# Sums and zero counts of the weights: from VectorE and GpSimd on one layout to ScalarE on another

## The chip, the cores and the metric

The kernel runs on one core of a Trainium2 chip, as a single program. The metric is the device time of one execution in microseconds (us). One execution was also recorded by the hardware profiler; its span runs from its first to its last instruction. PE is TensorE, DVE is VectorE, ACT is ScalarE, POOL is GpSimd, SP is the engine that issues most of the DMAs.

## The reference

A batch of 16 images with 256 channels of 28 x 28 goes through four layers, each with its input added at the end:

```python
# layer 0
out = _binary_activation(x)                       # values sign(x)
scaling = mean(abs(weights), axis=(1, 2, 3))      # one per output channel
y = conv3x3(out, sign(weights)) * scaling
x = batchnorm(y, gamma, beta) + x                 # moments over the batch
# layer 1
x = ...   # 3x3 and 1x1 convolutions of sign(x + move) with real weights (a_w, f_w),
          # PReLU, batch norms with given moments, two squeeze-and-excite gates
# layer 2
sf = mean(abs(w), axis=(1, 2, 3), keepdims=True)  # for w1 and for w2
out = sign(batchnorm(x, g1, b1))
out = prelu(conv3x3(out, sf1 * sign(w1)), a1)
out = sign(batchnorm(out, g2, b2))
out = prelu(conv3x3(out, sf2 * sign(w2)), a2)
x = prelu(batchnorm(out, g3, b3) + x, a3)
# layer 3
x = attention(x) + x                              # 784 tokens, 64 wide, softmax
```

The change concerns the three binary weight tensors, w0, w2a (`w1` of layer 2) and w2b (`w2` of layer 2), each 256 x 256 x 3 x 3. Of each the kernel needs the signs, the mean of |w| for every output channel (sf0, sf1, sf2, which enter the batch norms only through epsilon), and whether any weight is exactly zero: the fast path packs two output channels into one number and relies on signs of +1 and -1. If a zero or another doubt turns up, a flag makes the kernel run a second, careful path; with the inputs here it isn't run.

## The kernel before

Weights reach the chip as `taps`: for each half k of the input channels an array of 128 input channels by 9 taps by 256 output channels. They are loaded in six pieces of 128 x 768, (k, g), g being a row of taps.

`sign_weights` makes two lists of steps from them. A `sign` step lets ACT write the signs (L269, tile `sg`) and DVE pack two halves of the output channels into `wpk` (L270). An `add_up` step lets POOL compare the piece with zero and add the result up in `zeros` (L278, L279), and DVE sum |w| over the three taps (L285, tile `ab`) and add it to `sums` (L135, which is the line of a helper for all tensor_tensor operations). After the sixth piece, `total_up` sums over the partitions with two matmuls (L297, `sumabs`) and scales (L298). For layer 2 `both` joins a sign and an add_up step on the same piece.

`sign_layer` runs a binary convolution image by image, in an order written by hand on PE, ACT, DVE and SP. For image j: 36 matmuls (L350); signs of image j+1 into `fpads` on ACT (L461 in layer 0, L1051 in layer 2), with two pads in turn; bn_stats of image j-1 (L597, or PReLU and bn_stats at L1085 and L1087); then, from image 1 on, two entries of the list `steps`, one for each half image; then `apart`, in which ACT rounds the packed sums (L361, tile `t`) and takes the rounding off (L362), and DVE gets the other half by subtraction (L364, tile `n` in layer 0, `ab` in layer 2). PSUM has three buffers `cv`. The work that a step returns is run in the next slot, before that slot's own step.

In layer 0 the list holds: six `w1_step`s, which make layer 1's weights (DVE L511, L135 tile `asm`, L521; ACT L520, in turns), the `add_up` steps of w0 (whose six pieces stay in SBUF from the start), `fw_step`, `constants` (small DVE operations on the batch norms), and the six joint steps for w2a. Steps load their pieces two steps ahead into three buffers `x2`. In layer 2's first convolution the list holds the six joint steps for w2b.

Layer 1 is a loop `iteration(b)` over images, in hand-written order on PE, DVE and ACT; SP's order is the scheduler's. Per iteration PE takes a `cv` buffer six times: four pairs of 3x3 convolutions (L693) and two of the 1x1 convolution (L803). `rows_out` (DVE L733, tile `y`) empties the fourth pair. Near the end of an iteration ACT does two `squares2` (L834); at the start of the next it empties the 1x1 results (`unit_u`, L816, tile `u`). DVE's `branch2` (L825) and `transform` (L135, tile `vs`) stand between.

`doubts_so_far` (L1396 to L1399), near the end of layer 3, reduces `zeros` and the other doubts for the flag.

Of the kernel before, what the change touches and what calls it, by code (L numbers as in the profile page):

```python
# [27 lines left out]
F32 = mybir.dt.float32  # L28
FR = mybir.dt.float32r
F16 = mybir.dt.float16  # L30
BF16 = mybir.dt.bfloat16
# [8 lines left out]
P = 128  # L40
# [43 lines left out]
def forward(ctx: ExitStack, tc: tile.TileContext, d: dict, out: bass.AP, careful: bool):  # L84
# [42 lines left out]
    if not careful:  # L127
        zeros = const.tile([P, 3, 256], BF16, name="zeros")
        nc.gpsimd.memset(zeros, 0.0)
# [125 lines left out]
    def sign_weights(pool, dst, src, total, acc, stage=("st", 2), tmp=None, ab_tag="rn", sg=("sg", 1), deferred=None):  # L255


        sts, all_ = {}, []
        tmp = tmp or pool

        def load(k, g):
            if (k, g) not in sts:
                sts[k, g] = load_taps(pool, src, k, g, *stage)

        def sign(k, g):
            st = sts[k, g]
            n = CHUNKS.index((k, g))
            t = tmp.tile([P, 3, 256], BF16, tag=sg[0], name="sg", bufs=sg[1])
            A.activation(t, st, AF.Sign, saturate=False)  # L269
            return lambda: V.scalar_tensor_tensor(  # L270
                dst[:, n], t[:, :, P:], PACK, t[:, :, 0:P], ALU.mult, ALU.add
            )

        def add_up(k, g):
            st = sts.pop((k, g))
            if not careful:
                zero = const.tile([P, 3, 256], BF16, tag="zero", name="zero", bufs=1)
                nc.gpsimd.tensor_scalar(zero, st, 0.0, None, ALU.is_equal)  # L278
                nc.gpsimd.tensor_tensor(zeros, zeros, zero, ALU.add)  # L279
            if not all_:  # L280
                all_.append(tmp.tile([P, 256], F32, tag="total", name="sums", bufs=1))
                ab = all_[0]
            else:
                ab = tmp.tile([P, 256], F32, tag=ab_tag, name="ab", bufs=2)
            V.tensor_reduce(ab, st.rearrange("p t o -> p o t"), AX.X, ALU.add, apply_absolute_value=True)  # L285
            if ab is not all_[0]:
                tt(all_[0], all_[0], ab, ALU.add)
            if (k, g) == CHUNKS[-1]:
                if deferred is None:
                    return lambda: total_up()()  # L290
                deferred.append(total_up)
            return lambda: None

        def total_up():
            part = acc.tile([P, 2], F32, tag="sm", name="sumabs")
            for mo in range(2):
                T.matmul(part[:, mo:mo + 1], lhsT=all_[0][:, mo * P:(mo + 1) * P], rhs=ones, start=True, stop=True)  # L297
            return lambda: V.tensor_scalar(total, part, 1.0 / K9, None, ALU.mult)  # L298

        return [[Step(lambda c=c: load(*c), lambda c=c, f=f: f(*c)) for c in CHUNKS] for f in (sign, add_up)]  # L300

    def both(first, second):
        def work(f, s):
            rest = f.work(), s.work()
            return lambda: [r() for r in rest]

        return [Step(f.load, lambda f=f, s=s: work(f, s)) for f, s in zip(first, second)]
# [122 lines left out]
    with tc.tile_pool(name="ps_conv", bufs=3, space=PSUM) as psc, \  # L430
# [13 lines left out]
        with tc.tile_pool(name="ph1", bufs=1) as ph:  # L444
# [31 lines left out]
            signs, sums_ = sign_weights(ph, w0, d["w0"], sf0, pss, ("yu", 6), sg=("t1", 2))  # L476
# [106 lines left out]
            last_sum = []  # L583
            signs2, sums2 = sign_weights(xpool, w2a, d["w2a"], sf1, pss, ("x2", 3), tmp=ph, deferred=last_sum)
            steps = load_ahead(steps + both(signs2, sums2), 2)

            for i, x in enumerate(sums_):
                steps[3 * i + 1:3 * i + 1] = [x.work, None]
            steps[19:19] = [constants, None]
            steps[-5:-5] = [None]  # L590
            steps[-2:-2] = [None]
# [15 lines left out]

            with tc.manual_schedule(engines={ET.PE}):
                total_up = last_sum[0]()
# [23 lines left out]
            vs = ph.tile([P, 2, 4, 2, HR, S + 2], FR, tag="vs", name="vs")  # L633

# [211 lines left out]
            def iteration(b):  # L846
# [89 lines left out]
            with tc.manual_schedule(engines={ET.PE, ET.DVE, ET.Activation}):  # L936
# [13 lines left out]
                total_up()  # L950
# [83 lines left out]
        with tc.tile_pool(name="ph2", bufs=1) as ph:  # L1034
# [75 lines left out]
            steps = both(*sign_weights(xpool, w2b, d["w2b"], sf2, pss, ("x2", 3), tmp=ph, ab_tag="sums"))  # L1110
# [52 lines left out]
    attend_unshifted(tc, d, out, wqk, wv, wp, keys, worst, (doubts, zeros), flag, pv, finish)  # L1163
# [43 lines left out]
def attend_unshifted(ctx, tc, d, out, wqk, wv, wp, keys, worst, doubts, flag, pv, finish):  # L1207
# [510 lines left out]
```

## Time and profile before

| | us |
|---|---|
| median of 3 runs | 1015.17 |
| lowest and highest | 1012.84, 1019.25 |
| the profiled execution | 1017.7 |
| its span | 1015.4 |
| PE, DVE, ACT, POOL busy in the span | 972.5, 819.0, 632.4, 212.0 |
| layer 0 (start to the first matmul of layer 1) | 0 to 137.77 |
| layer 1 (to the first L350 of layer 2) | 137.77 to 509.37 |
| layer 2, first convolution | 509.37 to 621.99 |
| layer 2, second convolution | 621.99 to 734.03 |
| layer 3 | 734.03 to 1015.4 |

The stage borders are starts of matmuls in PE's timeline. The span is shorter than the execution's own time by 2.3 us. The busy time of PE is that of pipelined matmuls and doesn't say that it ran at its peak. The mean granted clock was 0.985 of full speed.

### The profile page before, as it was taken

What the parts mean: (1) busy time and instruction counts of PE and PEld (TensorE: products, weight loads), DVE (VectorE), ACT (ScalarE), POOL (GpSimd) and SP (SyncE); (2) the same over time, 40 slices, a digit from 0 to 9 for tenths busy, and PEclk for the clock granted to TensorE, in tenths of its full rate; (3) what the DMA queues carried; (4) which work ended last, traced back from release to release, by engine and by line L of the source; (5) the groups of instructions that cost most, each with busy time, mean ns of one, the idle gap of its engine ahead of it and who ended that gap; (6) DMA issues with size and microseconds to landing.
All of it is one profiled execution on the core that took longest, in us unless ns stands there. A gap on an engine that the chain in (4) does not pass through costs nothing. (4 is left out here: it accounts for less than half of the span.)

```text
span 1015.4 us, 14615 instructions
## 1 busy us (share of the span) xinstructions
PE 972.5 (96%) x5627; PEld 668.3 (66%) x5627; DVE 819.0 (81%) x1356; ACT 632.4 (62%) x1003; POOL 212.0 (21%) x186
## 2 busy tenths in 40 slices
PE   7898889999999999999999998999999999999996
PEld 3454569999999999999655554555444444444442
DVE  5997898998999998997769985888856776867775
ACT  5665444656566565665678865777576676666652
POOL 9423500000000000000043100000034444353521
PEclk9998999999999999999999999999999999999999
DMA  9666521222223222100194100000031534334312
GB/s 343 235 220 197 187 80 49 80 94 81 80 80 112 111 81 95 64 34 32 68 360 158 48 33 1 1 1 1 1 65 33 127 73 119 85 107 96 96 64 99
DMA packets 24354, 98.73 MB, mean 97 GB/s; under 512 B 3202, under 2 KB 6980, under 8 KB 24276
## 3 DMA queue, kind: packets, MB, share of 16 engines
q1 hardware_dynamic: 18356, 66.36, 18.5%
q0 software_dynamic: 5632, 30.54, 10.9%
q8 instruction: 46, 0.75, 0.3%
q10 hardware_dynamic: 288, 0.80, 0.2%
q14 instruction: 32, 0.26, 0.1%
HBM read 65.59 MB, written 32.11 MB: 96 GB/s over the span
## 5 line engine op out<-in xcount | busy, mean ns | idle before, releaser
L350 PE MATMUL cv<-fpads,wpk 128*128 128x392 f16 (+1 forms) x1746 | 304.3, 337 | 13.5 <-ACT fpads L1051 4.1
L693 PE MATMUL cv<-vs,w 128*128 128x392 f32 x1536 | 303.0, 355 | 3.0 <-DVE vs L135 3.0
L693 PEld LDWEIGHTS cv<-vs,w 128*128 128x128 f32 x1536 | 288.1, 191 | 5.8 <-issue 3.5
L350 PEld LDWEIGHTS <-wpk 128*128 128x128 f16 x1746 | 172.5, 99 | 145.3 <-issue 21.0
L1300 ACT ACTIVATE es<-sc 128x784 f32<-128x784 f32 x112 | 87.4, 822 | 41.9 <-PE sc L1296 41.7
L1296 PE MATMUL sc<-q,keyswa 64*128 64x392 f32 x448 | 89.9, 513 | 0.9 <-ACT es L1300 0.9
L831 POOL DMA_DIRECT2D x2d<-x x16 | 8.6, 536 | 359.9 <-DVE x L825 295.3
L1317 PE MATMUL av<-es,v 128*64 128x392 f32 x448 | 80.8, 499 | 0.0
L361 ACT ACTIVATE t<-cv,rounding 128x784 f32<-128x784 f32 (+2 forms) x52 | 44.6, 858 | 47.2 <-PE cv L350 46.5
L1085 DVE SCALAR_TENSOR_TENSOR p<-ab,vec 128x784 f32<-128x784 f32 (+1 forms) x68 | 69.4, 1020 | 1.2
L1310 POOL TENSOR_TENSOR sum<-sum,es 128x784 f32<-128x784 f32 x32 | 67.2, 2100 | 3.1 <-ACT es L1300 0.6
L1296 PEld LDWEIGHTS sc<-q,keyswa 64*128 64x128 f32 x448 | 38.9, 186 | 44.0 <-issue 17.1
L135 DVE TENSOR_TENSOR vs<-pad 128x840 fp32r<-128x840 bf16 (+1 forms) x66 | 64.4, 1000 | 0.1
L1317 PEld LDWEIGHTS av<-es,v 128*64 128x64 f32 x448 | 29.6, 136 | 47.1 <-issue 46.9
L364 DVE SCALAR_TENSOR_TENSOR ab<-ab,cv 128x784 f32<-128x784 f32 (+1 forms) x34 | 31.2, 917 | 36.3 <-ACT ab L362 36.3
L1284 DVE COPY keyswa<-mi 64x392 f32<-64x392 f32 x31 | 16.3, 565 | 52.6 <-ACT q L1280 52.6
L714 ACT ACTIVATE t<-cv,c_bn,s_bn 128x392 f32<-128x392 f32 x32 | 21.7, 678 | 52.9 <-PE cv L693 52.9
L803 PE MATMUL cv<-z,fw 128*128 128x392 f32 x256 | 49.1, 343 | 1.0 <-ACT z L795 0.9
L816 ACT ACTIVATE u<-cv,c_bn,s_bn 128x784 f32<-128x784 f32 x30 | 30.1, 1005 | 30.7 <-PE cv L803 30.6
L1308 POOL TENSOR_TENSOR sum<-es 128x784 f32<-128x784 f32 x16 | 30.0, 1878 | 91.0 <-ACT es L1300 91.0
L1273 PE MATMUL mi<-p,wqk 128*128 128x392 f32 x124 | 45.7, 509 | 2.2 <-DVE p L1260 2.1
L278 POOL TENSOR_SCALAR zero<-st 128x768 bf16<-128x768 f32 x18 | 39.2, 2179 | 40.5 <-DMA st<-in_w2b_dram 33.2
(287 smaller groups left out, 1531.9 us busy)
## 6 DMA issues: line engine op xcount, KB each, us to landing
xs<-in_x_dram SPq DMA_DIRECT2D x30, 784.0 KB, 4.4
x2d<-x POOLq DMA_DIRECT2D x16, 784.0 KB, 3.6
out_dram<-p SPq DMA_DIRECT2D x15, 784.0 KB, 3.5
p<-x2d POOLq DMA_DIRECT2D x14, 784.0 KB, 6.7
p<-x2d SPq DMA_DIRECT2D x13, 784.0 KB, 9.3
n0d<-n POOLq DMA_DIRECT2D x16, 392.0 KB, 4.2
n<-n0d SPq DMA_DIRECT2D x16, 392.0 KB, 3.0
st<-in_w_dram SPq DMA_DIRECT2D x12, 384.0 KB, 6.7
```

What stands on the lines that cost most here:

```text
L135: V.tensor_tensor(o, a, b, op)
L278: nc.gpsimd.tensor_scalar(zero, st, 0.0, None, ALU.is_equal)
L350: T.matmul(pss[j][:, n // size if careful else h, :rows * S].rearrange("p (a b) -> p a b", b=S), lhsT=w[:, n, t, :], rhs=pads[:, blocks[j] ...
L361: A.activation(by_halves(t, blocks[j]), ps, AF.Identity, bias=rounding, scale=1.0 / PACK)
L693: T.matmul(ps.rearrange("p (a b) -> p a b", b=S), lhsT=w[:, k, c, u, mo * P:(mo + 1) * P], rhs=vs[:, b % 2, u, k, :, c:c + S], start=(n == 0),
L803: T.matmul(ps[:, h, :HN], lhsT=w[:, k, mo * P:(mo + 1) * P], rhs=z2[b][:, k, h * HN:(h + 1) * HN], start=(k + i == 0), stop=(k + i == 2),)
L1085: V.scalar_tensor_tensor(p, y, alpha[:, mo:mo + 1], y, ALU.mult, ALU.max)
L1273: T.matmul(ps[:, h, :HN], lhsT=wqk[:, k, :], rhs=x[b][:, k, h * HN:(h + 1) * HN], start=(k == 0), stop=(k == 1))
L1296: T.matmul(ps[:, h, :HN], lhsT=chunk[rows], rhs=qs[b][rows], start=True, stop=True)
L1300: A.activation(e, ps[:, :, :HN], AF.Exp, scale=0.125)
L1310: (V if late else nc.gpsimd).tensor_tensor(sums[b, late], sums[b, late], e, ALU.add)
L1317: T.matmul(ps[64 * h:64 * h + 64, :HN], lhsT=w, rhs=e[:, h, :], start=start, stop=stop)
```

## The change

The weights are given to the chip a second time, as rows: two halves of 128 output channels by 2304. `weight_sums` loads them in six pieces of 128 x 768. On each, ACT computes |w| with an accumulator, which gives a sum for each output channel, and then the sign of the result, again with an accumulator, which counts the nonzero weights (`nonzero`, 18 columns). Both write over the piece. After the sixth piece DVE adds three partial sums per channel and scales. The comparison on POOL, the sums on DVE and the matmuls over partitions are gone.

The sums of w0 become steps of layer 0, which run in threes: a w1 step, a sum step of w0, a sign step of w2a. With the empty entries that are put in, an image with a w1 step and an empty slot alternates with an image that has a sum and a sign step, from image 1 to image 12; `fw_step` and `constants` follow at image 13. In before the w2a steps came after `fw_step` and `constants`. The sums of w2a and w2b are done in layer 1: iteration b loads a piece into one of two buffers `sts`, and iteration b+1 works on it, for b from 0 to 11, after the squares and before `transform`. The last piece of each tensor runs `add_up` on DVE at that place, in iterations 6 and 12.

In the compiled order SP issues the loads of the first two pieces of w2a's rows in layer 0. On POOL only the comparisons and additions are missing; the stores of `n` stand in the same order.

```diff
-    if not careful:
-        zeros = const.tile([P, 3, 256], BF16, name="zeros")
-        nc.gpsimd.memset(zeros, 0.0)
+    PIECE = K9 // 3
+    nonzero = None if careful else const.tile([P, 18], F32, name="nonzero")
...
-        def add_up(k, g):
-            st = sts.pop((k, g))
-            if not careful:
-                zero = const.tile([P, 3, 256], BF16, tag="zero", name="zero", bufs=1)
-                nc.gpsimd.tensor_scalar(zero, st, 0.0, None, ALU.is_equal)
-                nc.gpsimd.tensor_tensor(zeros, zeros, zero, ALU.add)
...
-            V.tensor_reduce(ab, st.rearrange("p t o -> p o t"), AX.X, ALU.add, apply_absolute_value=True)
-            if ab is not all_[0]:
-                tt(all_[0], all_[0], ab, ALU.add)
...
+        return [Step(lambda c=c: load(*c), lambda c=c: sign(*c)) for c in CHUNKS]
+
+    def weight_sums(room, src, total, at):
+        parts = const.tile([P, 2, 3], F32, name=f"abs_{at}")
+        sts = {}
+
+        def load(mo, q):
+            st = sts[mo, q] = room()
+            nc.sync.dma_start(out=st, in_=src[mo, :, q * PIECE:(q + 1) * PIECE])
+
+        def work(mo, q):
+            st = sts.pop((mo, q))
+            A.activation(st, st, AF.Abs, accum_out=parts[:, mo, q:q + 1])
             if not careful:
+                n = at + 3 * mo + q
+                A.activation(st, st, AF.Sign, accum_out=nonzero[:, n:n + 1])
+            if (mo, q) == (1, 2):
+                return add_up
             return lambda: None
 
-        def total_up():
-            part = acc.tile([P, 2], F32, tag="sm", name="sumabs")
-            for mo in range(2):
-                T.matmul(part[:, mo:mo + 1], lhsT=all_[0][:, mo * P:(mo + 1) * P], rhs=ones, start=True, stop=True)
-            return lambda: V.tensor_scalar(total, part, 1.0 / K9, None, ALU.mult)
...
+        def add_up():
+            V.tensor_reduce(total, parts, AX.X, ALU.add)
+            V.tensor_scalar(total, total, 1.0 / K9, None, ALU.mult)
...
-            signs2, sums2 = sign_weights(xpool, w2a, d["w2a"], sf1, pss, ("x2", 3), tmp=ph, deferred=last_sum)
-            steps = load_ahead(steps + both(signs2, sums2), 2)
-
-            for i, x in enumerate(sums_):
-                steps[3 * i + 1:3 * i + 1] = [x.work, None]
-            steps[19:19] = [constants, None]
-            steps[-5:-5] = [None]
-            steps[-2:-2] = [None]
+            def room_sums():
+                return xpool.tile([P, PIECE], F32, tag="x2", name="sts", bufs=3)
+
+            signs2, sums0 = sign_weights(xpool, w2a, d["w2a"], ("x2", 3), tmp=ph), weight_sums(room_sums, d["w0_rows"], sf0, 0)
+            steps = [s for three in zip(steps, sums0, signs2) for s in three] + steps[6:]
+            steps = load_ahead(steps, 2)
+            steps[19:19] = [constants]
+            for i in range(6):
+                steps[4 * i + 1:4 * i + 1] = [None]
...
-            with tc.manual_schedule(engines={ET.PE}):
-                total_up = last_sum[0]()
             keep_busy(28)
...
+            sums12 = weight_sums(room_sums, d["w2a_rows"], sf1, 6) + weight_sums(room_sums, d["w2b_rows"], sf2, 12)
...
                     load_x(b + 2, True)
+                if b < len(sums12):
+                    sums12[b].load()
...
                         squares2(b - 2, k)
+                if one and b <= len(sums12):
+                    sums12[b - 1].work()()
                 if ahead:
                     transform(b + 1, 0)
...
-            steps = both(*sign_weights(xpool, w2b, d["w2b"], sf2, pss, ("x2", 3), tmp=ph, ab_tag="sums"))
+            steps = sign_weights(xpool, w2b, d["w2b"], ("x2", 3), tmp=ph)
...
-        V.tensor_reduce(some, doubts[1], AX.XY, ALU.max)
-        V.scalar_tensor_tensor(sure, some, 0.0, sure, ALU.is_le, ALU.mult)
+        V.tensor_reduce(some, doubts[1], AX.X, ALU.min)
+        V.scalar_tensor_tensor(sure, some, K9 / 3.0, sure, ALU.is_ge, ALU.mult)
...
+        "w0_rows": get("L0_conv_weights").reshape(2, P, K9),
+        "w2a_rows": get(L2 + "w1").reshape(2, P, K9),
+        "w2b_rows": get(L2 + "w2").reshape(2, P, K9),
```

More of the change, by code (lines that the diff above doesn't have):

```diff
@@ L253, in load_ahead, with sign_weights @@
         return [lambda s=s, t=t: (s.work(), t.load() if t else None)[0] for s, t in zip(steps, steps[n:] + [None] * n)]
-    def sign_weights(pool, dst, src, total, acc, stage=("st", 2), tmp=None, ab_tag="rn", sg=("sg", 1), deferred=None):
-        sts, all_ = {}, []
+    def sign_weights(pool, dst, src, stage=("st", 2), tmp=None, sg=("sg", 1)):
+        sts = {}
         tmp = tmp or pool
         def load(k, g):
-            if (k, g) not in sts:
-                sts[k, g] = load_taps(pool, src, k, g, *stage)
+            sts[k, g] = load_taps(pool, src, k, g, *stage)
         def sign(k, g):
-            st = sts[k, g]
             n = CHUNKS.index((k, g))
             t = tmp.tile([P, 3, 256], BF16, tag=sg[0], name="sg", bufs=sg[1])
-            A.activation(t, st, AF.Sign, saturate=False)
+            A.activation(t, sts.pop((k, g)), AF.Sign, saturate=False)
             return lambda: V.scalar_tensor_tensor(
@@ L272, in sign @@
             )
-        def add_up(k, g):
-            st = sts.pop((k, g))
-            if not careful:
-                zero = const.tile([P, 3, 256], BF16, tag="zero", name="zero", bufs=1)
-                nc.gpsimd.tensor_scalar(zero, st, 0.0, None, ALU.is_equal)
-                nc.gpsimd.tensor_tensor(zeros, zeros, zero, ALU.add)
[L280 to L285, printed above, removed]
-            if ab is not all_[0]:
-                tt(all_[0], all_[0], ab, ALU.add)
[L288 to L291, printed above, removed]
-            return lambda: None
@@ L294, in total_up @@
-        def total_up():
-            part = acc.tile([P, 2], F32, tag="sm", name="sumabs")
-            for mo in range(2):
-                T.matmul(part[:, mo:mo + 1], lhsT=all_[0][:, mo * P:(mo + 1) * P], rhs=ones, start=True, stop=True)
-            return lambda: V.tensor_scalar(total, part, 1.0 / K9, None, ALU.mult)
[L300 to L307, printed above, removed]
+        return [Step(lambda c=c: load(*c), lambda c=c: sign(*c)) for c in CHUNKS]
@@ new lines, in weight_sums @@
+    def weight_sums(room, src, total, at):
+        parts = const.tile([P, 2, 3], F32, name=f"abs_{at}")
+        sts = {}
+        def load(mo, q):
[4 more added lines that the diff above has]
+            A.activation(st, st, AF.Abs, accum_out=parts[:, mo, q:q + 1])
+            if not careful:
+                n = at + 3 * mo + q
+                A.activation(st, st, AF.Sign, accum_out=nonzero[:, n:n + 1])
+            if (mo, q) == (1, 2):
+                return add_up
+            return lambda: None
+        def add_up():
+            V.tensor_reduce(total, parts, AX.X, ALU.add)
+            V.tensor_scalar(total, total, 1.0 / K9, None, ALU.mult)
+        return [Step(lambda c=c: load(*c), lambda c=c: work(*c)) for c in ((mo, q) for mo in range(2) for q in range(3))]
@@ L474, in room0 @@
                 return ns[b][:, :, r0 * S:(r0 + rows) * S]
-            signs, sums_ = sign_weights(ph, w0, d["w0"], sf0, pss, ("yu", 6), sg=("t1", 2))
+            signs = sign_weights(ph, w0, d["w0"], ("yu", 6), sg=("t1", 2))
             nc.gpsimd.memset(idle, 0.0)
@@ L582, in forward @@
             w2a = packed_weights(wpool, tag="wa2")
-            last_sum = []
-            signs2, sums2 = sign_weights(xpool, w2a, d["w2a"], sf1, pss, ("x2", 3), tmp=ph, deferred=last_sum)
-            steps = load_ahead(steps + both(signs2, sums2), 2)
-            for i, x in enumerate(sums_):
-                steps[3 * i + 1:3 * i + 1] = [x.work, None]
-            steps[19:19] = [constants, None]
-            steps[-5:-5] = [None]
-            steps[-2:-2] = [None]
+            def room_sums():
[6 more added lines that the diff above has]
+                steps[4 * i + 1:4 * i + 1] = [None]
             def post0(block, ab):
@@ L633, in forward, with room_sums @@
             vs = ph.tile([P, 2, 4, 2, HR, S + 2], FR, tag="vs", name="vs")
+            def room_sums():
+                return ph.tile([P, PIECE], F32, tag="sts", name="sts", bufs=2)
+            sums12 = weight_sums(room_sums, d["w2a_rows"], sf1, 6) + weight_sums(room_sums, d["w2b_rows"], sf2, 12)
             sums = {}
@@ L949, in forward @@
                     transform(0, u)
-                total_up()
                 for k in range(2):
@@ L1162, in forward @@
     keys = [wpool.tile([P, NC_, 4, 32], F32, tag=t, name=f"keys{t}") for t in ("wa", "wa2")]
-    attend_unshifted(tc, d, out, wqk, wv, wp, keys, worst, (doubts, zeros), flag, pv, finish)
+    attend_unshifted(tc, d, out, wqk, wv, wp, keys, worst, (doubts, nonzero), flag, pv, finish)
     return nc.values_load(flag[0:1, 0:1], min_val=0, max_val=P)
```

## The prediction

> **What bounds the kernel now.** I read the page's slices and engine shares first, then the timeline of the matmul engine (PE), because a PE at 96% busy can only lose time where it stands still, then VectorE (DVE) and ScalarE (ACT) beside each stop. The columns of a timeline are start, length, engine, line, what it does, and in brackets the idle time before it and who ended it. PE in layer 0, then in the first convolution of layer 2:
>
> ```profile
> 12.69 22.73 PE L350 MATMUL cv<-fpads,wpk 128*128 128x392 f16 x132 [1.28 <-DVE wpk L270]
> 38.59 38.51 PE L350 MATMUL cv<-fpads,wpk 128*128 128x392 f16 x216 [3.17 <-ACT fpads L461]
> 81.47 1.01 PE L297 MATMUL sumabs<-ones,sums 128*128 128x1 f32 x4 [4.37 <-DVE sums L135]
> 82.34 32.92 PE L350 MATMUL cv<-fpads,wpk 128*128 128x392 f16 x180
> 124.22 2.94 PE L350 MATMUL cv<-fpads,wpk 128*128 128x196 f16 x18 [3.06 <-DVE n L364]
> ...
> 598.34 0.61 PE L297 MATMUL sumabs<-ones,sums 128*128 128x1 f32 x4 [2.44 <-DVE sums L135]
> 598.81 14.02 PE L350 MATMUL cv<-fpads,wpk 128*128 128x392 f16 x72
> ```
>
> Undisturbed, the trace gives 6.12 us from image to image (36 matmuls), in layer 0 as in layer 2; 16 images would take 98 us. Layer 0 takes from 7.91 to 127.16. The two sumabs lines are PE standing in its queue behind a DVE sum. After the stops of 3.17, 4.37 and 2.44 us the image that follows takes 7.75, 8.28 and 7.75 us: the granted clock falls to 0.5 for a while.
>
> What paces layer 0 is the DVE/ACT loop around one image. From one "n" (L364) to the next:
>
> ```profile
> 49.46 0.96 DVE L364 SCALAR_TENSOR_TENSOR n<-n,cv 128x784 int16<-128x784 int16 x1
> 50.46 1.97 DVE L597 BATCH_NORM_STATS2 l_parts<-n 128x6 f32<-128x392 int16 x4
> 52.35 0.54 DVE L511 TENSOR_SCALAR st<-st 128x768 f32<-128x768 f32 x1
> ...
> 56.72 0.97 DVE L364 SCALAR_TENSOR_TENSOR n<-n,cv 128x784 int16<-128x784 int16 x1 [1.23 <-ACT n L362]
> 57.72 1.97 DVE L597 BATCH_NORM_STATS2 l_parts<-n 128x6 f32<-128x392 int16 x4
> 59.61 1.02 DVE L285 TENSOR_REDUCE ab<-st 128x256 f32<-128x768 f32 x1
> 60.66 0.42 DVE L135 TENSOR_TENSOR sums<-sums,ab 128x256 f32<-128x256 f32 x1
> 61.00 0.96 DVE L364 SCALAR_TENSOR_TENSOR n<-n,cv 128x784 int16<-128x784 int16 x1
> ```
>
> An image with a w1 step takes 7.26 us, though DVE waits 1.23 us in it: ACT does its w copies only as DVE delivers, and then t and n. With w1 and a sum it is 7.34 (42.12 to 49.46): the sum lay in that wait. An image with a sum alone takes 4.28.
>
> Layer 1 is different: PE is busy 278.36 of the 280 us from 220 to 500. One iteration is 21.96 us, of PE work alone. The slack around the place of the new work:
>
> ```profile
> 307.04 1.02 DVE L825 SCALAR_TENSOR_TENSOR x<-u,gates,x 128x784 f32<-128x784 f32 x1
> 307.99 1.97 DVE L135 TENSOR_TENSOR vs<-pad 128x840 fp32r<-128x840 bf16 x2
> 309.88 1.15 DVE L733 SCALAR_TENSOR_TENSOR y<-cv,s_bn,uvs 128x392 f32<-128x392 f32 x2
> ...
> 308.11 0.95 ACT L834 ACTIVATE square<-x,shift 128x784 f32<-128x784 f32 x1 [0.96 <-DVE x L825]
> 308.97 0.18 ACT L834 ACTIVATION_READ_ACCUMULATOR square<-x,shift 128x1 f32 x1
> 310.73 1.01 ACT L816 ACTIVATE u<-cv,c_bn,s_bn 128x784 f32<-128x784 f32 x1 [1.58 <-PE cv L803]
> ...
> 311.91 6.99 PE L693 MATMUL cv<-vs,w 128*128 128x392 f32 x36
> ```
>
> ACT is free for 1.58 us before the u step; the y step ends 0.9 us before PE starts the next iteration.
>
> **What the Trainium skill says.** "SBUF — State Buffer", section "SBUF: two separate sides": GpSimd and a DVE operation with two SBUF inputs share a port pair under an exclusive lock, and the loser blocks. The trace agrees: the two asm additions take 0.76 us as a rule but 2.20 us at 33.05 and 72.27, each time beside a GpSimd add of zeros (33.32 and 72.53). "TensorE: Matmul & The Clock Gate", Part 1: about 3.4 us idle bring the clock to half. Here the stops from 2.4 us up did, those of 1.06 and 1.28 us did not. "ScalarE: Activation LUTs", "What ACT_TABLE_LOAD costs": a pointer operand adds some 93 ns to an ACTIVATE, and neighbours overlap by that much. The trace has 0.95 us for 784 elements with a bias tile, 0.84 without, and 0.09 overlap. Its section "Table sets" has abs in every set; the changed program indeed holds no further table load.
>
> **The change part by part.**
>
> *Price of a piece.* No Abs or Sign with an accumulator is in the trace. Nearest row: Sign of 128x768 (L269), 0.84 us, plus a read of the accumulator as after square, 0.19, less 0.1 overlap: 0.93, and 1.95 for the pair with its in-place dependence. Bounds: 1.6 (as two fpads signs, 1.59, with both reads hidden) to 2.4 (as dear as square, 0.95, with nothing overlapped).
>
> *Layer 0, start.* The zeros work leaves GpSimd, so the third and fourth wpk (10.65, 2.45 us together, against an add of zeros at 10.57) take 0.55 each. PE's stop of 1.28 goes; next late is image 1's input (ACT waits for its DMA until 14.80) and its two signs. I take 0.8 us: n of image 0 at 18.3. Bounds 0 and 1.3.
>
> *Layer 0, loop.* In pairs now: a w1 image, then an image with Abs, Sign and sg on ACT. The w1 image: 7.26 plus wpk before it, 0.55 less 0.08 overlap: 7.73. The other is ACT's own queue from the end of its n: two fpads 1.50, Abs and Sign 1.95 less 0.1, sg 0.75, t 0.81, n 0.98: 5.8. A pair 13.5 against 12.24 of PE. So ACT/DVE pace it, and PE stops some 1.4 us at every second image, too short for the clock. From 18.3: image 1 at 25.6 (no wpk yet), image 2 at 31.4, five pairs, image 12 at 98.9 (before: 105.30). Image 13 carries fw and the constants: 2.89 (n, bn), 0.47, and the 7.1 of before (85.49 to 92.60) less 0.35 for l_e, which is earlier, and 1.4 for v_bn, which took 1.68 beside GpSimd: 8.7, at 107.6. Image 14: 2.89 and the aggregates 1.65: 112.2. From there DVE works through bn and the last three parts: 1.0 + 1.9 + 0.5 + 1.0 and twice 0.98, 6.4 in all: 118.6 against 132.61 before. The six late image steps with sg, reduce and sum, and the wait for sumabs, are gone. Extra loads: six pieces of w0 and two of w2a, 384 KB each, 3.1 MB; per pair of images all traffic is some 3.6 MB in 13.5 us, 265 GB/s, where 349 was moved from 12 to 30 us. The three buffers give each load about 7 us for a landing of 3.6 to 6.7. I take 0.5 for it: gain 13.5. The first n load of layer 1 waits for image 14's store: n + 8.3 (store begun 1.3 later, landed 3.7 after, load 3.0), 120.5, where layer 1 first wants it at 120.4. No gain is lost, but no more could be had cheaply.
>
> *Layer 1.* Twelve pairs, one an iteration, 1.95 us after the squares: 309.15 plus 1.75 to u is 310.9 instead of 310.73. DVE wants u only at 313.82, PE's bank 4.7 us later: nothing. Their loads, 17 GB/s, go beside a DMA share of 0.21. But in iterations 6 and 12 the sum is finished at once: DVE's reduce stands behind the Abs just issued. DVE is ready at 308.07, the Abs read ends at 310.05, reduce and scale take until 310.4, and then vs and y follow: y ends 2.4 us later, at 313.4. The next pair of convolutions takes the PSUM buffer that y frees (three buffers, six takings an iteration), so PE starts at 313.45 instead of 311.91: 1.55 us, twice: +3.1. Bounds 0 (if another buffer is free) and 5. DVE's own idle time, 1.2 us after the g sums, takes up the rest. The small sf operations removed at the start of layer 1 stood beside PE's full queue: nothing.
>
> *Layer 2.* Six reduces and five adds, 8.3 us of DVE, and GpSimd's zeros go. DVE then has about 10.7 us for two images of 12.24, so only sumabs' stop ends: 598.81 to 595.73 is 3.07, and the slow image 1.63: 4.7. The aggregates then come 0.6 late on DVE before image 14's ab: gain 4.1. Bounds 3 and 4.7.
>
> *End.* The reduce over zeros, 0.94, becomes one over 18 columns, about 0.15. PE waits 0.39 for the DVE work behind it, and is then next late itself: 0.4.
>
> Sum: -13.5 + 3.1 - 4.1 - 0.4 = -14.9. The profiled run took 1017.7 (span 1015.4): 1002.8. The median shown, 1015.17, lies 2.5 lower and would give 1000.3. I say 1001.5.
>
> **Rivals.**
> - *PE bound in layer 0.* If ACT hides the sums, layer 0 runs at 6.12 an image: 15.7 + 15 x 6.12 = 107.5, last bn at 110.2, 22.4 gained, in all -23.8: 992. For it: ACT is busy only 76.67 of the first 137.5 us. Against it: t and n stand behind the new pair in the same queue.
> - *The new loop is longer.* Each pair of images pays about 1 us more (the pair at 2.4 us, a load landing late behind an x load), six times, and layer 1's wait 5 instead of 3.1: 1009. For it: DMA is dense at 30 to 90 us (share 0.63 and 0.73).
> - *Layer 1's ScalarE queue.* The twelve pairs come out in the open, because u and the sign behind it set the next PE work: 12 x 1.95 = 23.4 more, 1025 or, with DVE drawn in, somewhat over: slower than before. It decides from 1.25 us an iteration, where it eats the 14.9. Against it: the slack of 1.58 before u, and u's takers come 2.7 us later.
>
> **How the numbers follow.** Forecast 0.62 (own range 997 to 1006); PE-bound layer 0 0.08; longer loop 0.26; layer 1's queue 0.04. The range 994 to 1010 runs from near the PE-bound case to the longer loop. About 1% is what a measurement of this kernel tells from no change: faster means below 1005. From the cases: 0.60 + 0.08 + 0.05 faster, 0.73; 0.24 the same, a part of the last rival among them; 0.03 slower.
>
> **What would show it.** The profile after should have: no sumabs and no zero rows; asm pairs always near 0.76; n of image 12 near 99 and a first layer 1 matmul near 123.5 (before 137.77); images in layer 0 alternating 7.7 and 5.8 us; PE stops near 1.5 us at iterations 6 and 12 of layer 1 and none at the other ten; layer 2's first convolution without a stop. An Abs far from 0.84, a stop on a DMA in layer 0, or iterations of layer 1 longer than 21.96 would make it wrong.

## The result, and the profile after

The changed kernel takes 999.4 us (median of 4 runs, 998.23 to 999.90), the kernel before on the same chip 1014.43 us (1012.84 to 1019.25): a ratio of 0.984, with an interval of 0.981 to 0.988. The profiled executions lie further apart, 998.2 against 1017.7. In 23 runs on another chip the kernel before spread from 1011.2 to 1020.7 around 1014.9, so its profiled execution is a long one. The medians moved by 15.0 us, the profiled spans by 18.9, so a stage of the profile before can be some 2 to 3 us longer than usual.

By stage, from the starts of matmuls in TensorE's timeline, in us:

| stage | before | after | moved | forecast |
|---|---|---|---|---|
| layer 0 | 137.77 | 124.34 | -13.43 | -13.5 |
| layer 1 | 371.60 | 371.41 | -0.19 | +3.1 |
| layer 2, first convolution | 112.62 | 108.52 | -4.10 | -4.1 |
| layer 2, second convolution | 112.04 | 111.43 | -0.61 | 0 |
| layer 3 | 281.37 | 280.80 | -0.57 | -0.4 |

In the eleven experiments below, the second convolution of layer 2 took 111.4 to 113.0 us and layer 3 took 280.5 to 282.6, with no order in it by what was edited. Differences under 2 us in these two stages are therefore not read as effects, and the experiments are read by the other three stages.

TensorE's timeline after, in layer 0 and in layer 2's first convolution:

```profile
15.61 36.87 PE L340 MATMUL cv<-fpads,wpk 128*128 128x392 f16 x216 [0.18 <-ACT fpads L451]
53.29 12.40 PE L340 MATMUL cv<-fpads,wpk 128*128 128x392 f16 x72 [0.81 <-ACT fpads L451]
66.83 12.40 PE L340 MATMUL cv<-fpads,wpk 128*128 128x392 f16 x72 [1.14 <-ACT fpads L451]
80.37 12.40 PE L340 MATMUL cv<-fpads,wpk 128*128 128x392 f16 x72 [1.14 <-ACT fpads L451]
...
112.88 1.71 PE L340 MATMUL cv<-fpads,wpk 128*128 128x196 f16 x18 [0.81 <-DVE n L354]
...
496.95 97.56 PE L340 MATMUL cv<-fpads,wpk 128*128 128x392 f16 x573 [0.52 <-ACT fpads L1047]
```

There is no sumabs line any more. In layer 0 TensorE now starts two images every 13.54 us (from 53.29 to 66.83 to 80.37), with a stop of 1.14 us each time for ScalarE's signs. The images after such a stop aren't slow: the 72 matmuls of two images take 12.40. The first convolution of layer 2 runs through without a stop.

The loop around one pair of images, on ScalarE (first fence) and on VectorE (second):

```profile
48.73 0.42 ACT L510 ACTIVATE w<-st 128x256 fp32r<-128x256 f32 x1 [2.48 <-DVE st L501]
...
51.54 0.95 ACT L352 ACTIVATE n<-t,unrounding 128x784 int16<-128x784 f32 x1
52.40 1.59 ACT L451 ACTIVATE fpads<-xs 128x784 f16<-128x784 f32 x2
53.89 0.83 ACT L285 ACTIVATE sts<-sts 128x768 f32<-128x768 f32 x1
54.63 0.19 ACT L285 ACTIVATION_READ_ACCUMULATOR sts<-sts 128x1 f32 x1
54.84 0.84 ACT L288 ACTIVATE sts<-sts 128x768 f32<-128x768 f32 x1
55.59 0.19 ACT L288 ACTIVATION_READ_ACCUMULATOR sts<-sts 128x1 f32 x1
55.69 0.83 ACT L266 ACTIVATE sg<-st 128x768 bf16<-128x768 f32 x1
```

```profile
44.79 0.97 DVE L354 SCALAR_TENSOR_TENSOR n<-n,cv 128x784 int16<-128x784 int16 x1 [2.82 <-ACT n L352]
...
52.53 0.97 DVE L354 SCALAR_TENSOR_TENSOR n<-n,cv 128x784 int16<-128x784 int16 x1 [1.23 <-ACT n L352]
53.53 1.97 DVE L588 BATCH_NORM_STATS2 l_parts<-n 128x6 f32<-128x392 int16 x4
58.33 0.97 DVE L354 SCALAR_TENSOR_TENSOR n<-n,cv 128x784 int16<-128x784 int16 x1 [2.83 <-ACT n L352]
```

Abs, Sign and their two reads take from 53.89 to 55.69, where sg begins: 1.80 us. From n to n the w1 image takes 7.74 and the image with the sum 5.80. The line to remember is the first one: in the w1 image ScalarE stands for 2.48 us until VectorE delivers.

Layer 1, VectorE in iteration 6, where the sum of w2a is finished:

```profile
272.27 0.08 DVE L818 DVE_READ_ACCUMULATOR x<-u,gates,x 128x1 f32 x1
274.28 0.16 DVE L294 TENSOR_REDUCE sf<-abs 128x2 f32<-128x6 f32 x1 [1.94 <-ACT sts L285]
...
276.44 1.15 DVE L726 SCALAR_TENSOR_TENSOR y<-cv,s_bn,uvs 128x392 f32<-128x392 f32 x2
```

The wait of VectorE for the Abs is there, 1.94 us, and y ends at 277.6. But TensorE doesn't stop:

```profile
273.32 3.03 PE L796 MATMUL cv<-z,fw 128*128 128x392 f32 x16
276.19 7.06 PE L686 MATMUL cv<-vs,w 128*128 128x392 f32 x36
```

It starts the next pair of convolutions at 276.19, before y has even begun.

### The profile page after: what moved, and what is told of

Read it like the earlier page. It is cut to its first block, busy times and chain, and to the rows that moved or that the text cites. A ratio compares the mean times of both kernels' runs of the same rounds, so it can differ in the third digit from the quotient of the medians.

```text
span 996.5 us, 14562 instructions
## 1 busy us (share of the span) xinstructions
PE 962.4 (97%) x5609; PEld 664.2 (67%) x5615; DVE 781.8 (78%) x1326; ACT 661.3 (66%) x1075; POOL 141.0 (14%) x149
## 4 chain that ended last, share of the span: by engine, by line
PE 44%; DVE 4%; ACT 2%; issue 0%; DVEq 0%; ACTq 0%
PE cv L340 17%; PE sc L1292 8%; PE av L1313 8%; PE mi L1269 5%; PE sm L1355 2%; PE mi L1373 2%; DVE p L1081 1%; PE sm L1313 1%; DVE ab L354 1%; DVE l2b_fin L1083 1%; DVE l2c_fin L1083 1%; ACT es L1296 0%; ACT fpads L1047 0%; DVE r L1339 0%; PE sc L1269 0%
## 5 line engine op out<-in xcount | busy, mean ns | idle before, releaser
L340 PE MATMUL cv<-fpads,wpk 128*128 128x392 f16 (+1 forms) x1746 | 297.3, 332 | 12.3 <-ACT fpads L451 5.2
L340 PEld LDWEIGHTS <-wpk 128*128 128x128 f16 x1746 | 169.5, 97 | 140.6 <-issue 13.9
L1081 DVE SCALAR_TENSOR_TENSOR p<-ab,vec 128x784 f32<-128x784 f32 (+1 forms) x68 | 66.5, 978 | 1.2
L796 PEld LDWEIGHTS cv<-z,fw 128*128 128x128 f32 x256 | 45.9, 188 | 2.2 <-ACT z L788 2.2
L432 PE MATMUL unused<-idle 128*128 128x512 bf16 x170 | 39.9, 391 | 3.3 <-POOL idle L468 3.0
```

Source lines behind the costliest of these rows:

```text
L340: T.matmul(pss[j][:, n // size if careful else h, :rows * S].rearrange("p (a b) -> p a b", b=S), lhsT=w[:, n, t, :], rhs=pads[:, blocks[j] ...
L796: T.matmul(ps[:, h, :HN], lhsT=w[:, k, mo * P:(mo + 1) * P], rhs=z2[b][:, k, h * HN:(h + 1) * HN], start=(k + i == 0), stop=(k + i == 2),)
L1081: V.scalar_tensor_tensor(p, y, alpha[:, mo:mo + 1], y, ALU.mult, ALU.max)
```

## Layer 1: why the stop didn't come, and what the pairs cost

My theory: TensorE went on because of one choice of a buffer. In the compiled order, the first pair of convolutions after iterations 6 and 12 waits for ScalarE (the u step), after the others up to 11 for VectorE (the y step). The three PSUM buffers seem to be handed out by when the planner, which lays out the program as it is compiled, expects them to come free, and it had seen the late y. The rival: VectorE's wait is absorbed with any buffer. The edit takes the buffers in a fixed turn.

```diff
+        turn = [0]
         def conv_ps():
-            return psc.tile([P, 2, 512], F32, tag="cv", name="cv")
+            turn[0] += 1
+            return psc.tile([P, 2, 512], F32, tag=f"cv{turn[0] % 3}", name="cv", bufs=1)
```

> The changed kernel, with the three PSUM buffers cv taken in a fixed turn. In the changed kernel the plan gives the first pair of convolutions after iterations 6 and 12 the buffer that the u step empties; in a fixed turn it gets the one that y empties, as in the other iterations. My theory: the +3.1 us that I forecast for layer 1 failed on this choice of a buffer alone. Then TensorE stands still twice, from 276.2 to the end of y at 277.5 and the same in iteration 12: 1.3 us each, layer 1 goes from 371.4 to 374.0 us and the span from 996.5 to about 999.1. Rival: VectorE's wait of 1.94 us for the Abs would be hidden with any buffer; then both iterations stay at 21.97 and the span at 996.5.

Layer 1 took 374.21 us, 2.80 more. TensorE's timeline at iteration 6 and, below it, a line of its list of waits in layer 1 (us in total, times, longest):

```profile
272.57 3.03 PE L799 MATMUL cv<-z,fw 128*128 128x392 f32 x16
276.89 7.08 PE L689 MATMUL cv<-vs,w 128*128 128x392 f32 x36 [1.29 <-DVE y L729]
```

```profile
PE cv L689 <- DVE y L729: 2.6, 2, 1.3
```

Two stops of 1.3 us, in the two iterations and nowhere else. The theory stands, as far as it says that the buffer decides; how the planner chooses is inferred. In the compiled order of the kernel before, the same pair takes u's buffer after iterations 2 to 14 and y's only after the first two. The span came out at 1001.3, because layer 3 and the second convolution of layer 2 were 2.6 longer in that execution and layer 0 was 0.6 shorter; the median is 1002.39.

How near ScalarE's queue in layer 1 is to deciding (the rival on the slower side) was tried by tripling the pairs, with their extra sums thrown away:

```diff
+            for _ in range(2 if at and not careful else 0):
+                A.activation(st, st, AF.Abs, accum_out=spare[:, 0:1])
+                A.activation(st, st, AF.Sign, accum_out=spare[:, 1:2])
             if (mo, q) == (1, 2):
                 return add_up
```

> The changed kernel, with each pair Abs and Sign of layer 1 followed by two more pairs on the same piece whose sums are thrown away: 5.5 us of ScalarE an iteration in place of 1.84. My theory: ScalarE's queue has waits of 1.2, 1.5, 0.25 and 1.2 us behind the u steps, and VectorE some 1.2 us of idle time, so TensorE stays the bound or nearly so: 0 to 0.5 us an iteration, layer 1 371.4 to 377.4, span 996.5 to 1002.5. Rival (ScalarE's queue in layer 1 decides, the case on the slower side): all that is added comes out in the open, 12 x 3.7 = 44 us, span near 1040; with the first pair hidden and nothing beyond it, 12 x 2.5 = 30, near 1026.

Layer 1 took 381.26, 9.85 more, in a span of 1007.6: more than my 6, far less than the rival's 30 to 44. TensorE's timeline at iteration 6 and at an ordinary one:

```profile
280.84 8.48 PE L690 MATMUL cv<-vs,w 128*128 128x392 f32 x36 [2.04 <-DVE y L730]
...
304.27 6.99 PE L690 MATMUL cv<-vs,w 128*128 128x392 f32 x36
```

Iterations 6 and 12 grew from 22.02 to 25.65, 7.3 together: with u this late the compiled order gives the pair y's buffer in these two iterations as well, so the stop that I had forecast for the changed kernel is here, 2.04 us, and a slower clock after it (8.48 against 6.99 for the same 36 matmuls). The other ten iterations paid 0 to 0.32 us each for 3.7 us more of ScalarE, 1.7 in all, and 0.9 lies in the first matmuls of the layer, ahead of any pair. So the queue had room: a single pair costs nothing, and two more cost an ordinary iteration less than a tenth of their length.

## Layer 0: whose work it was

The forecast sum for layer 0 was met, but it didn't say which part of the change paid. Three runs take the two old works out of the kernel before, one at a time and together.

```diff
-                zero = const.tile([P, 3, 256], BF16, tag="zero", name="zero", bufs=1)
-                nc.gpsimd.tensor_scalar(zero, st, 0.0, None, ALU.is_equal)
-                nc.gpsimd.tensor_tensor(zeros, zeros, zero, ALU.add)
+                pass
```

> The kernel before, with GpSimd's comparison of the weights with zero and its addition left out (no weight is looked at for zeros); the sums stay on VectorE. My theory: this takes away what VectorE loses beside GpSimd, and no more: the third and fourth wpk (2.45 to 1.1 us), two pairs of asm (2.20 to 0.76 each), v_bn (1.68 to 0.23) and the step on stf (1.03 to 0.42). Layer 0 becomes 3 to 6 us shorter (first matmul of layer 1 near 133), layer 2's first convolution keeps its stop at sumabs and its 112.6 us: span 1010.5 (1009 to 1012.5). So at most a third of the 13.4 us won in layer 0 is GpSimd's. Rival 1: these operations stand in waits for ScalarE or TensorE anyway: layer 0 keeps 137.8 and the span 1015. Rival 2: GpSimd's sums are the greater part: layer 0 below 131.

Layer 0 took 128.95, 8.8 less: my 3 to 6 was too low, and the second rival (below 131) came true. The span was 1005.5, the ratio 0.989 (0.987 to 0.991). VectorE's timeline of the first w1 image in this run:

```profile
23.50 0.75 DVE L519 SCALAR_TENSOR_TENSOR w<-asm,w 128x256 fp32r<-128x256 f32 x2
24.17 0.41 DVE L519 SCALAR_TENSOR_TENSOR w<-st,w 128x256 fp32r<-128x256 f32 x1
24.50 1.02 DVE L283 TENSOR_REDUCE sums<-st 128x256 f32<-128x768 f32 x1
25.81 0.97 DVE L362 SCALAR_TENSOR_TENSOR n<-n,cv 128x784 int16<-128x784 int16 x1 [0.29 <-ACT n L360]
```

and the same operations in the kernel before:

```profile
24.62 2.20 DVE L521 SCALAR_TENSOR_TENSOR w<-asm,w 128x256 fp32r<-128x256 f32 x2
26.74 1.54 DVE L521 SCALAR_TENSOR_TENSOR w<-st,w 128x256 fp32r<-128x256 f32 x1
28.20 1.02 DVE L285 TENSOR_REDUCE sums<-st 128x256 f32<-128x768 f32 x1
29.14 0.95 DVE L364 SCALAR_TENSOR_TENSOR n<-n,cv 128x784 int16<-128x784 int16 x1
```

I had listed wpk, asm, v_bn and the step on stf as what stood beside GpSimd and missed this place: from n to n that image took 10.00 us and takes 7.26 without GpSimd's work. The images at 29 and 68 us give 1.4 each. The one at 105 us gives 2.1, of which 1.7 is a wpk that took 2.23 beside GpSimd and takes 0.55. The image with the constants gives only 0.2, though v_bn falls from 1.68 to 0.23: VectorE waits for ScalarE's n there. The start gives 0.6. The slowing is what the Trainium skill says in "SBUF — State Buffer", section "SBUF: two separate sides", of the port pair that VectorE and GpSimd share under a lock: the VectorE operations that grew here have two SBUF inputs and GpSimd was at work beside them (2.20 against 0.75), while the reduce, with one input, is 1.02 us in both. One input alone is no safeguard, though: the step on stf, which has one, took 1.03 us beside GpSimd and takes 0.41 without it.

```diff
-            if not all_:
-                all_.append(tmp.tile([P, 256], F32, tag="total", name="sums", bufs=1))
...
-            V.tensor_reduce(ab, st.rearrange("p t o -> p o t"), AX.X, ALU.add, apply_absolute_value=True)
-            if ab is not all_[0]:
-                tt(all_[0], all_[0], ab, ALU.add)
...
-                T.matmul(part[:, mo:mo + 1], lhsT=all_[0][:, mo * P:(mo + 1) * P], rhs=ones, start=True, stop=True)
-            return lambda: V.tensor_scalar(total, part, 1.0 / K9, None, ALU.mult)
+            return lambda: V.memset(total, 0.01)
```

> The kernel before with VectorE's sums of |w| and the two sumabs matmuls left out (the scales are set to a constant), and GpSimd's work on zeros kept: the complement of the run without the zero work. My theory: the two overlap little. Layer 0 falls by 4.6 us (13.4 less the 8.8 that GpSimd's part measured), to 133.2 (131.5 to 135), since GpSimd still stops VectorE beside it; layer 2's first convolution loses its stop and takes 108.5 to 109.5. Span 1006.5. Rival: VectorE's sums fill the same waits as GpSimd's locks; then either alone gives most of it, and layer 0 falls to 128.

Layer 0 took 126.07, 11.7 less, not 4.6: my theory fell, and the rival (128) is nearer. Layer 2's first convolution took 108.52, as in the changed kernel, so leaving out VectorE's sums and their stop is enough for its whole 4.1 us. With both works out (the two edits together):

> The kernel before with both GpSimd's work on zeros and VectorE's sums with their matmuls left out (no zeros are looked for, the scales are a constant), and nothing put in their place. The runs that left out one of them shortened layer 0 by 8.8 and 11.7 us. My theory: they overlap, and together give less than the 20.5 of their sum, since TensorE's 6.12 an image becomes the bound up to image 9 and the chain of sg and wpk keeps the last images at 7.6 to 7.8: layer 0 at 121 (119 to 124), against 124.34 in the changed kernel, which does the same work on ScalarE in another order. Rival: they add up, 117.3.

Layer 0 took 121.17, as forecast: 16.6 less, where the two alone gave 8.8 and 11.7. The first matmul of layer 1 before, without GpSimd's work, without VectorE's sums, and without both:

```profile
137.77 10.78 PE L693 MATMUL cv<-vs,w 128*128 128x392 f32 x48 [3.01 <-DVE vs L135]
128.95 7.25 PE L691 MATMUL cv<-vs,w 128*128 128x392 f32 x24 [3.03 <-DVE vs L135]
126.07 4.14 PE L682 MATMUL cv<-vs,w 128*128 128x392 f32 x13 [4.18 <-DVE vs L135]
121.17 9.08 PE L680 MATMUL cv<-vs,w 128*128 128x392 f32 x36 [5.84 <-DVE vs L135]
```

The three differences share one profiled execution of before, so a stretch that happened to be long in it is counted twice when two of them are added. The medians of the whole kernel say the same, though: 10.6 and 12.7 alone, 17.6 together. The two works fill in part the same waits, so neither "the gain of GpSimd" nor "the gain of VectorE" is a fixed number, and a difference of two runs (13.4 less 8.8, my 4.6) isn't the price of what is left.

## Layer 0: engine or order

The changed kernel with layer 0's steps in the order of before, the sums on ScalarE:

```diff
-            steps = [s for three in zip(steps, sums0, signs2) for s in three] + steps[6:]
+            steps = [s for two in zip(steps, sums0) for s in two] + steps[6:] + signs2
             steps = load_ahead(steps, 2)
-            steps[19:19] = [constants]
             for i in range(6):
-                steps[4 * i + 1:4 * i + 1] = [None]
+                steps[3 * i + 2:3 * i + 2] = [None]
+            steps[19:19] = [constants, None]
+            steps[-5:-5] = [None]
+            steps[-2:-2] = [None]
```

> The changed kernel with layer 0's steps in the order of the kernel before (w1, sum, empty; then fw, constants, and the six sign steps of w2a), the sums of w0 still on ScalarE. It tells the change of engine from the change of order. My theory: three images cost 9.1 (w1, then sum: the pair stands behind the w copies, in the open), 7.26 and 5.1, 21.5 where the new order takes 20.3, and the images from 10 on, which hold only fw, constants and sign steps, run at 4.6 to 7.3 off TensorE's lead: last bn near 117 against 118.2, first matmul of layer 1 at 123 to 124.3. So the order by itself is worth nothing (within 1.5 us), and the engine is all of the gain. Rival: the new order is the gain in layer 0; then the old one gives 128 or more.

The loop came out as forecast, 9.06, 7.26 and 5.07 us from n to n, nine images long. The end did not: images 13 to 15 took 7.60, 7.80 and 5.48 where I had 4.6 to 7.3, and the first matmul of layer 1 came at 130.96. So my theory fell, and the order is worth 6.6 of the 13.4 us. ScalarE's list of waits from 95 to 135 us says why, for this kernel and, in the same window, for the kernel before:

```profile
ACT sg L266 <- DVE wpk L267: 11.8, 5, 3.7
```

```profile
ACT sg L269 <- DVE wpk L270: 14.6, 5, 3.7
```

A sign step writes the one buffer sg, and has to wait until VectorE has packed the piece before it, which it does after bn. Where two sign steps fall in one image, t and n stand behind that chain. The new order puts one sign step into every second image, and the chain is gone: from 20 to 135 us ScalarE has no such wait in the changed kernel. If that is what the order is worth, a second buffer is worth as much. The old order, with the sums on ScalarE and two sg:

```diff
-    def sign_weights(pool, dst, src, stage=("st", 2), tmp=None, sg=("sg", 1)):
+    def sign_weights(pool, dst, src, stage=("st", 2), tmp=None, sg=("sg", 2)):
```

> The version with the old order of layer 0's steps and the sums on ScalarE, with two buffers sg in place of one. There the last images take 7.6 and 7.8 us because each sign step waits for VectorE's wpk of the step before to empty the one buffer sg (waits of ScalarE of 2.0, 3.7 and 3.5 us). My theory: that single buffer is most of what the order is worth in layer 0; with two, images 13 to 15 take about 5, 6.6 and 4.9, and the first matmul of layer 1 comes at 126.5 (125 to 128.5) in place of 130.96. Rival: the 9.06 us images (the pair behind the w copies) carry the difference to 124.34, and two buffers give less than 1 us.

The first matmul of layer 1 in the old order, in the old order with two sg, and in the changed kernel:

```profile
130.96 0.43 PE L688 MATMUL cv<-vs,w 128*128 128x392 f32 x1 [4.18 <-DVE vs L134]
124.31 6.02 PE L688 MATMUL cv<-vs,w 128*128 128x392 f32 x23 [3.35 <-DVE vs L134]
124.34 10.76 PE L686 MATMUL cv<-vs,w 128*128 128x392 f32 x48 [3.71 <-DVE vs L134]
```

The median is 998.83. My theory holds and its price was too low: images 13 to 15 take 6.13, 5.04 and 3.63. For the length of layer 0, then, the old order with a second sg and the new order are the same.

The same buffer in the kernel before, with nothing else changed:

> The kernel before, with two buffers sg in place of one and nothing else. In its list of waits ScalarE waits 14.6 us in five times for wpk to empty sg, and VectorE in turn waits 1.29, 1.29, 1.28 and 0.64 us for the n of images 12 to 15. My theory: these 4.5 us of VectorE are what a second buffer can give there, since VectorE's reduces and sums fill the rest of the same time: layer 0 from 137.8 to 133.8 (133.3 to 135), span 1011.5. Rival 1: the full 6.65 us that it gave with the sums on ScalarE: 131.1. Rival 2: GpSimd's lock takes it back: 137.

Layer 0 took 132.71 in the profiled execution, 5.1 less, of which images 13 to 15 are 2.9, while 2.4 lie in the images up to 8, which the edit doesn't touch. Over 20 runs against 23 the ratio is 0.9981 (0.9966 to 0.9995), 1.8 us. So a second sg helps there, but less than with the sums on ScalarE: VectorE's reduces fill the time that it frees. Single executions show 5.1 and medians 1.8: the spread of the kernel before once more. It also bears on the sections above: of each gain in layer 0 that is measured from the one profile of before (8.8, 11.7, 16.6 and the change's own 13.4), up to 2.4 us may be that execution's.

## A faster order

ScalarE's wait of 2.48 us in the w1 image is longer than the pair of 1.80. If the sum stands ahead of the w1 step, it should vanish in that wait:

```diff
-            steps = [s for three in zip(steps, sums0, signs2) for s in three] + steps[6:]
+            steps = [s for three in zip(sums0, steps, signs2) for s in three] + steps[6:]
...
-                steps[4 * i + 1:4 * i + 1] = [None]
+                steps[4 * i + 2:4 * i + 2] = [None]
```

> The changed kernel, with the two parts of a pair of images in layer 0 put together otherwise: the sum of w0 stands in the w1 image ahead of the w1 step, and the other image keeps the sign step of w2a alone. My theory: a w1 image has 2.48 us in which ScalarE waits for VectorE's first w1 operation, and the pair Abs and Sign (1.84 us) fits in there, so the w1 image stays at 7.74 us, the other one falls from 5.80 to 4.0 by the loop, and a pair of images (11.7) goes below TensorE's 12.24. Images come at 6.12 on average up to image 12, whose n moves from 98.94 to about 94.9; image 13 with fw and the constants keeps its 8.7, and the first matmul of layer 1 comes about 4 us earlier, near 120. Span 992.5 (991 to 994). Rival: it is the sum of ScalarE's work that paces the pair, wherever it stands; then the w1 image grows to 9.6, the other falls to 4.0, the pair stays at 13.5 and the span at 996.5.

ScalarE's timeline, and TensorE's through layer 0:

```profile
43.65 0.83 ACT L285 ACTIVATE sts<-sts 128x768 f32<-128x768 f32 x1
44.39 0.19 ACT L285 ACTIVATION_READ_ACCUMULATOR sts<-sts 128x1 f32 x1
44.60 0.84 ACT L288 ACTIVATE sts<-sts 128x768 f32<-128x768 f32 x1
45.35 0.19 ACT L288 ACTIVATION_READ_ACCUMULATOR sts<-sts 128x1 f32 x1
46.23 0.42 ACT L510 ACTIVATE w<-st 128x256 fp32r<-128x256 f32 x1 [0.68 <-DVE st L501]
```

```profile
15.69 91.98 PE L340 MATMUL cv<-fpads,wpk 128*128 128x392 f16 x558 [0.19 <-ACT fpads L451]
...
117.51 10.76 PE L686 MATMUL cv<-vs,w 128*128 128x392 f32 x48 [3.81 <-DVE vs L134]
```

The wait shrank from 2.48 to 0.68 us, the w1 image stayed at 7.73, a pair of images fell to 12.23, and TensorE works from 15.69 to 107.67 without a stop. This is the case "PE bound in layer 0" of the prediction, reached with all the work kept. Layer 0 is 6.8 us shorter than in the changed kernel; before this run I had forecast 4, with n of image 12 at 94.9 where it came at 91.23. The median is 992.95, the ratio to the kernel before 0.977 (0.975 to 0.978).

What is left then is image 13 with fw_step and constants (8.32 us) and a wait of 1.95 us for the load of n. Two versions go on from here. One moves fw_step and constants into empty slots of images 10 and 4 (the edit is shown against the changed kernel):

```diff
-            steps = [s for three in zip(steps, sums0, signs2) for s in three] + steps[6:]
+            fw_last = steps.pop()
+            steps = [s for three in zip(sums0, steps, signs2) for s in three]
+            steps[14:14] = [fw_last]
             steps = load_ahead(steps, 2)
-            steps[19:19] = [constants]
             for i in range(6):
-                steps[4 * i + 1:4 * i + 1] = [None]
+                if i != 4:
+                    steps[4 * i + 2:4 * i + 2] = [constants if i == 1 else None]
```

> The version with the sums ahead of the w1 steps, and fw_step and constants taken from image 13 into empty slots of earlier images (10 and 4), so that image 13 carries nothing. My theory: layer 0 is then TensorE's alone to its end (107.6); n of image 14 comes at 103.3 instead of 104.14, the last bn ends near 109.5 instead of 110.5, but the load of n for layer 1 waits for the store of image 14 and lands only 0.8 earlier: first matmul of layer 1 at 116.7 (117.51 before), span 991.4. Rival: constants, some 4.4 us of VectorE in one image, pushes the loop so far that TensorE stops for a PSUM buffer: nothing gained or up to 2 us lost.

The first matmul of layer 1 came at 116.54 (forecast 116.7), but not as I had it: TensorE does stop once, for 1.12 us at 90.71, and finishes layer 0 later, at 109.3. It waits there for ScalarE's signs, not for a PSUM buffer as the rival had it, and behind image 10, which now holds fw_step (6.51 us from n to n where it took 4.51); the constants ran long before, at 41 to 44 us. In return VectorE no longer waits for n, and TensorE stands only 1.23 us ahead of layer 1 instead of 3.81:

```profile
116.54 9.31 PE L688 MATMUL cv<-vs,w 128*128 128x392 f32 x48 [1.23 <-DVE vs L134]
```

so its first 48 matmuls take 9.31 us and not 10.76 (the granted clock over them is 1.00 and not 0.84), and layer 1 is 370.0 in place of 371.4. The median is 990.21, the ratio 0.975 (0.972 to 0.978). The other version adds a third buffer n:

```diff
-                    ns[b] = ph.tile([P, 2, N], I16, tag="n", name=f"n{b}", bufs=2)
+                    ns[b] = ph.tile([P, 2, N], I16, tag="n", name=f"n{b}", bufs=3)
...
-                return ph.tile([P, PIECE], F32, tag="sts", name="sts", bufs=2)
+                return ph.tile([P, PIECE], F32, tag="sts", name="sts", bufs=1)
...
```

> As the version with fw_step and constants moved, and with three buffers n instead of two (to make room, the pieces of the sums in layer 1 have one buffer instead of two and are loaded after the work on the piece before). My theory: what is late last ahead of layer 1 is the load of n, which waits for the store of image 14 out of the same buffer (VectorE waits 1.95 us for it where the sums come first, 0.99 in the changed kernel). With a third buffer it waits for image 13 only and is there by 106, so the first matmul of layer 1 comes 2 to 3 us earlier, at 114.5, span 989.2. The later loads cost nothing in layer 1 (371.4). Rival: the x image loaded beside it is as late: then 116.7 and 991.4.

First matmul of layer 1 at 116.33, median 990.49: nothing gained. The wait that it was to remove had already gone with the step before it. These two are the fastest measured, 9 us under the changed kernel.

## Why the prediction was right, and where not

*Price of a piece.* 1.80 us against 1.95: right, and the bounds hold.

*Layer 0, start.* n of image 0 at 18.18 (forecast 18.3): right as a number. That it comes of GpSimd's work is not shown: in the kernel before with two sg, which keeps that work, n of image 0 came at 18.18 too.

*Layer 0, loop.* n of image 1 at 25.45 (25.6), 2 at 31.25 (31.4), 12 at 98.94 (98.9), 13 at 107.27 (107.6), 14 at 111.85 (112.2), last bn until 118.2 (118.6); w1 image 7.74 (7.73), sum image 5.80 (5.8). Following one engine's queue from release to release gave the loop to a tenth, with some luck: the terms of the sum image (1.50, 1.85, 0.75, 0.81, 0.98) add up to 5.89 and not to 5.8, and this slip offset the pair priced too dear. The DMA allowance of 0.5 shows up not in the loop but at its end, as a wait of 0.99 us for the load of n that I had called just in time. The gain of 13.5 puts the first matmul of layer 1 at 124.27, not at the 123.5 that the prediction names beside it; it came at 124.34. Where the prediction names two stops that left the clock alone, 1.06 and 1.28 us, the profile before has none of 1.06; its stops under 1.28 are of 0.93 us at most. What the working missed is the cause's split: it never priced GpSimd by itself (8.8 us alone) and didn't read the chain of sg and wpk as a wait that a buffer could have removed.

*Layer 1.* Ten of the twelve pairs cost nothing: right. The other two are the step that failed: "The next pair of convolutions takes the PSUM buffer that y frees". It took the one that u frees, as it does after 13 of 15 iterations in the kernel before. The 1.94 us of VectorE's wait were right, and so was the price where the sentence holds: 2.8 us with the buffers in a fixed turn against the 3.1 forecast. The bound of 0 "if another buffer is free" was the answer.

*Layer 2.* 4.10 against 4.1. The parts are less sure than the sum: in the run without GpSimd's work the same stop at sumabs (2.41 us) cost no slow image, and the stage took 110.96. The 1.63 us of slow clock are there in the profile before and in that of before with two sg (112.61), and not in this one; why is open.

*End.* The wait of 0.39 us is gone; the stage's 0.57 is within its spread.

*The sum.* Against the profiled execution -14.9 was 3.3 short in layer 1 and 0.6 in a stage where I had expected nothing. Against the medians, which moved by 15.0, the nearness is partly luck: the 3.1 us of loss in layer 1 that didn't come offset a profiled execution of before that was longer than most. Of the rivals, PE bound in layer 0 is not what happened but could have been had; the longer loop and layer 1's queue did not come about.

## What to carry to other kernels

Before work is moved to another engine, look for the waits in that engine's own queue, and put the work ahead of the instruction that waits: the same Abs and Sign cost 1.3 us a pair of images in the one image and nothing in the wait of the other. When one edit takes several works away, the gains of leaving them out one at a time don't add up, so price each by a run of its own before crediting it. And where a step rests on which buffer a tile gets, read that from the compiled waits: where a release was late, the compiled order here handed out another one.

## What was not expected of the hardware

The granted clock of TensorE did not follow the length of its stops. The share granted over the image or the 36 matmuls that follow, from the windows of the traces: 1.00 after a stop of 1.29 us (fixed turn), 0.80 after 2.04 (tripled pairs), 1.00 after 2.41 (no zero work, at sumabs in layer 2), 0.77 after 2.44 (before, at the same place), 0.78 after 2.41 (before with two sg, at the same place). The Trainium skill, "TensorE: Matmul & The Clock Gate", Part 1, has about 3.4 us of idle time bring the clock down; here stops of 2.0 and 2.4 us did so, and one of 2.4 did not. Two of the windows:

```profile
591.00:596.50 5.50, 5.50 (x34) 3.18 (x33) 5.50 (x11) 1.69 (x5) 0.00 (x0) 1.00 0.00 0
```

```profile
598.90:606.30 7.40, 7.40 (x36) 3.81 (x35) 6.83 (x14) 1.93 (x5) 0.00 (x0) 0.77 0.00 0
```

(The first is the run without the zero work, the second the kernel before; PEclk is the third number from the end.) The page says that activity is watched in a window that runs freely, so that the place of a stop in it could matter; no run here tests that, and it stays open. In their profiles the kernel before has seven stops of 2 to 4.4 us from its first convolution to the start of layer 3, the changed kernel has three; in 4 runs each on the same chip the one spread over 6.4 us, the other over 1.7. That the stops make the spread is not shown. In the 23 runs of before the clock goes with the time in part: the longest run of before, 1020.74, had a mean clock of 0.983, the shortest, 1011.17, had 0.988, but another at 0.983 took 1013.14.
